# Stores of turned blocks on GpSimd, four unit buffers in the attention's first part, and adds in pieces

## The chip, the cores and the metric

The kernel runs on one core of one Trainium2 chip. The metric is device time in microseconds of one execution. A core has five engines that run side by side, each with a queue that it takes in order: TensorE (PE in the profile; it multiplies matrices, and PEld is its load of weights), VectorE (DVE), ScalarE (ACT), GpSimd (POOL) and SyncE (SP), which computes nothing and issues most transfers. Sixteen DMA engines move the data; a transfer is issued by an engine's queue, and whoever needs the data waits for its landing.

## The reference

The input x has two sequences of 2048 rows with 256 features. The layer normalises each row, and adds three things: x itself, causal attention with one head, and a feed-forward net (FFN) on the same normalised rows.

```
xn = layernorm(x)
q, k, v = xn @ Wq, xn @ Wk, xn @ Wv
out  = softmax(causal(q k^T) / 16) v @ Wo
h = silu(xn @ w1 * s1) * (xn @ w2 * s2)
h = gelu(h @ h1 * s_h1);  h = gelu(h @ h2 * s_h2)
y = x + out + (h @ w3) * s3
```

The FFN's weights hold only -1, 0 and 1 before scaling. The hidden width is 1024.

## The kernel before

**Stages.** The rows are cut into eight blocks of 512 rows (n = 0 to 7; 0 to 3 are the first sequence), and each block into four tiles of 128 rows, (n, t). The program first does the attention of all tiles, and then the FFN in four rounds of two blocks. The hidden layers of the FFN use a Strassen-like scheme of seven products each, with factors that are prepared beside the attention and kept in DRAM. Each number is carried as a high and a low part.

**A tile of the attention.** `score` (L410) multiplies the queries of a tile with the keys of each block m and moves the result to s in SBUF (L434, VectorE), and ScalarE takes the exponential (L446). These values, P, must then be turned, with the keys on partitions, before `weigh` (L505) multiplies them with the values (high parts in L518, low parts in L523) into the output bank po. There are two banks po. VectorE empties a bank into r at L537, and the next but one tile needs it.

**How P is turned.** Units of at most eight key tiles (UK = 8) go through DRAM when there are at least five key tiles in the unit (`by_blocks`, L458); smaller ones are transposed by TensorE (L490). For a unit that goes through DRAM:

1. `turn_blocks` (L305): VectorE transposes 32x32 blocks of the unit into one of two buffers b (L308), and SP stores b in DRAM as d (L313). The next but one turn waits until that store has landed, since it writes the same b.
2. `fetch_blocks` (L316): SP fetches d back with its blocks in another order, in four transfers (L320), into a buffer e. There are two buffers e, in the pool bp.
3. `turn` (L470): ScalarE casts a part of e to the high part of pT (L484), and VectorE or GpSimd subtracts it for the low part (L486; GpSimd when m is odd). There are four buffers pT.

`fetch_units` (L463) decides when a fetch is written into the program: when the first part of a unit is turned, it fetches that unit, if that is not done, and one more. The normalised x of the second sequence is turned the same way (`turn_keys`, L351), after GpSimd has normalised it (L345), 16 steps of 128 rows, in one go. Its results are the keys k (L363, L364), stored as xT_d (L365).

**Beside the attention.** Weights of the FFN are looked at, one item after another: ScalarE issues their loads, and GpSimd (L136), VectorE and ScalarE work on them. First come w1 and w2, then the signs of h2 (`item_signs`), then the factors of h1 (`item_factors`). The factors' sums are formed in xh0, a buffer of 128 x 2048 numbers that is not used earlier in the attention, and later holds the FFN's first input.

**The FFN.** A round calls `square` for h1 and for h2. After product 3 of h2, `rests_of` (L1004) loads the attention's result and x for two blocks, and GpSimd adds them (L1015), one add of 128 x 1024 numbers for each block. The last step (L1051) adds the FFN's output to that and SP stores the sum.

**Order.** The program is written in the order above, but the instructions of an engine do not stand in that order: a scheduler puts them in the order in which it expects them to become ready. `tc.issue_after(mark)` binds the instructions inside it that run on the mark's own engine to stand behind the mark; it waits for nothing. So a change in one place can move instructions of the other engines too.

Of the kernel before, what the change touches and what calls it, by code (L numbers as in the profile page):

```python
# [9 lines left out]
F32 = mybir.dt.float32  # L10
F32R = mybir.dt.float32r
# [4 lines left out]
ALU = mybir.AluOpType  # L16
# [49 lines left out]
def attn_ffn_kernel(  # L66
# [124 lines left out]
    with ExitStack() as actx:  # L191
# [6 lines left out]
        sp = actx.enter_context(tc.tile_pool(name="sp", bufs=3))  # L198
        bp = actx.enter_context(tc.tile_pool(name="bp", bufs=2))
        ptp = actx.enter_context(tc.tile_pool(name="ptp", bufs=LEAD + 2))  # L200
        small = actx.enter_context(tc.tile_pool(name="small", bufs=4))
# [3 lines left out]
        xs, rstds, ks, qs, vs = {}, {}, {}, {}, {}  # L205
        turns = {"ps": 0, "b": 0, "q": 0}

        def in_turn(key, tiles):
            turns[key] += 1
            return tiles[(turns[key] - 1) % len(tiles)]  # L210

        def bank():
# [92 lines left out]
        def turn_blocks(src, k, name):  # L305

            b = in_turn("b", b_tiles).rearrange("p i t -> p (i t)")[:, : k * P]
            nc.vector.transpose(  # L308
                b.rearrange("p (g k q) -> p k g q", g=P // Q, q=Q),
                src.rearrange("p (k g q) -> p k g q", g=P // Q, q=Q),  # L310
            )
            d = dram.tile([P, k * P], F32, name=f"d_{name}")
            nc.sync.dma_start(out=d, in_=b)  # L313
            return d
# [147 lines left out]

        def fetch_units(until, more):  # L463
            while units and (more or until not in fetched):
                more = more and until not in fetched
                n, t, u, k, d = units.pop(0)
                e = bp.tile([P, UK * P], F32, tag="e", name=f"e_{n}_{t}_{u}")[:, : k * P]
                fetched[n, t, u] = fetch_blocks(d, k, e)

        def turn(n, t, m):  # L470
# [3 lines left out]
            w = tiles * P  # L474
            pT = ptp.tile([P, 2, TB], F32R, tag="pT", name=f"pT_{n}_{t}_{m}")
            state[n, t][m] = pT
            if by_blocks(n, t, m):
                u, at = divmod((m - first) * NT, UK)
                fetch_units((n, t, u * UK), at == 0)
                src = fetched[n, t, u * UK][:, ds(at, tiles)]  # L480
                hi, lo = (
                    pT[:, a, :w].rearrange("p (k i q) -> p k i q", k=tiles, q=Q) for a in range(2)
# [146 lines left out]

        def item_signs(src):  # L630
            items.append(([src], [(0, lambda t: odd(t[0]))]))

# [17 lines left out]
        for k in range(HC):  # L650
            item_signs(h2[:, k, :])
        for c in range(HK):
# [132 lines left out]
    def ffn_ternary(actx):  # L785
# [83 lines left out]
        def square(layer, n, B, sets, last, beside):  # L869
# [6 lines left out]
            def product(step, out, start):  # L876
# [3 lines left out]
                for o in range(HK):  # L880
                    for c in range(HK):
                        for a in range(2):
                            nc.tensor.matmul(  # L883
                                out=out[o], lhsT=w[:, c, ts(o, P)], rhs=sets[right][c][:, a, :],
                                start=(start and c == 0 and a == 0), stop=(c == HK - 1 and a == 1),
                                skip_group_check=True,
                            )
                if step in beside:
# [57 lines left out]
            return C, nxt  # L946

        raw_h2 = {}

# [54 lines left out]
        def rests_of(n):  # L1004
# [4 lines left out]
            )  # L1009
            rests = {}  # L1010
            for i, m in enumerate((n + 1, n)):
                rests[m] = rest = rt[:, ts(i, NT), :]
                nc.sync.dma_start(out=rest, in_=r_d[m].rearrange("p (t d) -> p t d", d=D))
                nc.sync.dma_start(out=xt[:, ts(i, NT), :], in_=rows_of(m))
                nc.gpsimd.tensor_tensor(rest, rest, xt[:, ts(i, NT), :], ALU.add)  # L1015
            return rests

# [5 lines left out]
        for n in range(0, N, 2):  # L1023
# [6 lines left out]
            B, sets = square("h1", n, B, sets, False, later)  # L1030
            rests = {}
            B, sets = square("h2", n, B, sets, True, {3: lambda: rests.update(rests_of(n))})
            for m in (n + 1, n):
# [221 lines left out]
```

## Time and profile before

| what | us |
|---|---|
| median of 3 runs (866.09 to 869.82) | 868.33 |
| the profiled execution's own time | 868.75 |
| its span | 866.9 |
| first gated matmul of the FFN (the attention's end) | 262.2 |
| TensorE busy | 849.5 |
| GpSimd busy | 234.7 |

Busy time is the time in which an engine has an instruction in it. Matmuls overlap, so a busy TensorE is not TensorE at its peak; a gap between the starts of two matmuls that is longer than the columns of the first shows better what is lost. A bracket behind an instruction in the timeline gives the idle time of its engine before it and what ended it. The landing of a transfer is counted from its issue.

### The profile page before, as it was taken

What the parts mean: (1) busy time and instruction counts of PE and PEld (TensorE: products, weight loads), DVE (VectorE), ACT (ScalarE), POOL (GpSimd) and SP (SyncE); (2) the same over time, 40 slices, a digit from 0 to 9 for tenths busy, and PEclk for the clock granted to TensorE, in tenths of its full rate; (3) what the DMA queues carried; (4) which work ended last, traced back from release to release, by engine and by line L of the source; (5) the groups of instructions that cost most, each with busy time, mean ns of one, the idle gap of its engine ahead of it and who ended that gap; (6) DMA issues with size and microseconds to landing.
All of it is one profiled execution on the core that took longest, in us unless ns stands there. A gap on an engine that the chain in (4) does not pass through costs nothing.

```text
span 866.9 us, 12257 instructions
## 1 busy us (share of the span) xinstructions
PE 849.5 (98%) x4298; PEld 720.5 (83%) x4298; DVE 644.1 (74%) x1123; ACT 498.7 (58%) x881; POOL 234.7 (27%) x178
## 2 busy tenths in 40 slices
PE   9999799999999999999999999999999999999997
PEld 7988688988888878878988888988888898888887
DVE  6689685887965799986596596479478648848764
ACT  3456665655655466676257576436557635557671
POOL 3022823111111666630142150026024003502300
PEclk9999999999999999999999999999999999999999
DMA  8987899667881998754234444433444431144411
GB/s 276 361 233 233 249 314 291 222 234 231 286 283 51 389 403 282 285 194 152 93 132 143 144 146 141 144 116 109 145 145 145 145 135 58 49 146 146 146 49 53
DMA packets 62678, 162.51 MB, mean 187 GB/s; under 512 B 6545, under 2 KB 36369, under 8 KB 53265
## 3 DMA queue, kind: packets, MB, share of 16 engines
q1 hardware_dynamic: 57792, 145.14, 48.6%
q10 hardware_dynamic: 3728, 12.32, 4.6%
q0 software_dynamic: 1088, 4.19, 1.3%
q8 instruction: 36, 0.59, 0.3%
q14 instruction: 34, 0.27, 0.1%
HBM read 120.21 MB, written 47.71 MB: 194 GB/s over the span
## 4 chain that ended last, share of the span: by engine, by line
PE 83%; DVE 6%; DMA 5%; issue 2%; POOL 1%; ACT 1%; SPq 1%; DVEq 0%; ACTq 0%; POOLq 0%
PE ps_own L883 22%; PE ps L883 21%; PE ps L425 7%; PE ps L174 6%; PE ps_own L174 6%; PE po L518 4%; PE ps_own L1044 4%; PE ps L1044 4%; PE ps L398 3%; DMA e<-d 3%; DMA d<-b 2%; PE po L523 2%; PE ps L382 1%; POOL x L345 1%; DVE h_T L188 1%
## 5 line engine op out<-in xcount | busy, mean ns | idle before, releaser
L425 PE MATMUL ps<-k,q 128*128 128x512 f32 (+3 forms) x480 | 109.0, 366 | 0.4 <-ACT q L264 0.4
L425 PEld LDWEIGHTS ps<-k,q 128*128 128x128 f32 x480 | 82.0, 189 | 13.4 <-ACT q L264 1.2
L518 PE MATMUL po<-v,pT 128*128 128x512 f32 x272 | 79.1, 401 | 6.5 <-ACT pT L484 4.7
L486 POOL TENSOR_TENSOR pT<-e,pT 128x512 fp32r<-128x512 f32 (+3 forms) x30 | 36.8, 1229 | 140.1 <-ACT pT L484 102.6
L1015 POOL TENSOR_TENSOR rt<-rt,xt 128x1024 f32<-128x1024 f32 x8 | 21.9, 2758 | 170.3 <-issue 114.8
L904 ACT ACTIVATE k_h_u<-k_h_u,h_s_sb 128x512 f32<-128x512 f32 x64 | 45.9, 723 | 36.6 <-DVE k_h_u L903 36.0
L446 ACT ACTIVATE s<-s,low 128x1024 f32<-128x1024 f32 (+7 forms) x48 | 42.9, 895 | 30.8 <-DVE low L440 30.6
L518 PEld LDWEIGHTS po<-v,pT 128*128 128x128 f32 x272 | 47.3, 189 | 14.3 <-ACT pT L484 5.5
L863 POOL TENSOR_TENSOR k_h_u<-k_h_p,k_h_u 128x512 f32<-128x512 f32 x16 | 23.3, 1459 | 122.1 <-ACT q L187 106.0
L484 ACT CAST pT<-e 128x512 fp32r<-128x512 f32 (+3 forms) x60 | 32.8, 574 | 38.8 <-DMA e<-d 26.9
L434 DVE TENSOR_SCALAR_CACHE_REDUCE s<-ps 128x512 f32<-128x512 f32 (+3 forms) x80 | 47.2, 598 | 5.0 <-PE pt L490 3.1
L523 PEld LDWEIGHTS po<-v,pT 128*128 128x128 f32 x272 | 42.4, 188 | 6.8 <-DVE pT L486 0.7
L523 PE MATMUL po<-v,pT 128*128 128x256 f32 x272 | 46.2, 283 | 0.1
L188 DVE TENSOR_TENSOR q<-k_h_u,q 128x512 fp32r<-128x512 f32 x32 | 43.4, 1384 | 0.0
L308 DVE STREAM_TRANSPOSE b<-s 128x1024 f32<-128x1024 f32 (+3 forms) x30 | 33.4, 1124 | 8.3 <-ACT s L446 4.8
L922 POOL TENSOR_TENSOR k_h_p<-f_h_B,k_h_p 128x512 f32<-128x512 f32 x16 | 32.6, 2065 | 20.0 <-DVE h_h_T L188 20.0
L174 PE MATMUL ps<-xh,w_sb 128*128 128x512 f32 x144 | 36.4, 391 | 0.8 <-ACT b L182 0.8
L863 POOL TENSOR_TENSOR f_w_B<-f_w_B,f_w_B 128x512 f32<-128x512 f32 x16 | 26.8, 1692 | 33.1 <-DVE f_w_B L183 33.1
L903 DVE TENSOR_TENSOR k_h_u<-ps_own,k_h_u 128x512 f32<-128x512 f32 x32 | 21.7, 686 | 17.5 <-PE ps_own L883 17.4
L904 ACT ACTIVATE k_h_p<-k_h_p,h_s_sb 128x512 f32<-128x512 f32 x32 | 22.8, 722 | 19.3 <-DVE k_h_p L903 19.3
L903 DVE TENSOR_TENSOR k_h_u<-ps,k_h_u 128x512 f32<-128x512 f32 x32 | 22.0, 690 | 14.3 <-PE ps L883 14.3
L174 PE MATMUL ps<-xh1t,w_sb 128*128 128x512 f32 x128 | 31.8, 389 | 0.0
(178 smaller groups left out, 2206.2 us busy)
## 6 DMA issues: line engine op xcount, KB each, us to landing
w_h_S<-factors_h SPq DMA_DIRECT2D x32, 1024.0 KB, 4.8
w_h_A<-factors_h SPq DMA_DIRECT2D x24, 1024.0 KB, 4.8
d<-b SPq DMA_DIRECT2D x18, 512.0 KB, 3.9
e<-d SPq DMA_DIRECT2D x72, 128.0 KB, 3.2
xT_d<-k SPq DMA_DIRECT2D x8, 1024.0 KB, 6.0
stg<-in_ffn_h_w ACTq DMA_DIRECT2D x16, 512.0 KB, 4.8
r_d<-r SPq DMA_DIRECT2D x8, 512.0 KB, 4.3
factors_h<-xh SPq DMA_DIRECT2D x4, 1024.0 KB, 4.5
```

Of the source, the lines that this page charges most:

```text
L174: nc.tensor.matmul(out=p, lhsT=w[:, c, ts(o, P)], rhs=xh[:, c, a, :], start=(c == 0 and a == 0), stop=(c == DC - 1 and a == 1),)
L188: nc.vector.tensor_tensor(r[:, 1, :], f, r[:, 0, :].bitcast(F32), ALU.subtract)
L425: nc.tensor.matmul(out=ps[:, :w], lhsT=qs[n][:, c, a, ts(t, P)], rhs=ks[m][:, c, b, :w], start=(k == 0), stop=(m < n and k == 3 * DC - 1),)
L434: marks["DVE"] = nc.vector.tensor_scalar(st["s"][:, ds(at, w)], ps[:, :w], 1.0, None, ALU.mult, ALU.max, accum_out=st["tops"][:, m - first ...
L446: marks["ACT"] = nc.scalar.activation(st["s"][:, at], st["s"][:, at], AF.Exp, bias=low, accum_out=st["sums"][:, u // UK : u // UK + 1],).ins
L518: nc.tensor.matmul(out=st["po"], lhsT=pT[:, 0, ts(j, P)], rhs=vs[m][:, j, :, :], start=(m == first and j == 0), stop=False,)
L523: marks["PE"] = nc.tensor.matmul(out=st["po"][:, 0, :], lhsT=pT[:, 1, ts(j, P)], rhs=vs[m][:, j, 0, :], start=False, stop=(m == n and j == ...
L863: nc.gpsimd.tensor_tensor(B["B12"][i], B["B22"][i], B["B12"][i], ALU.subtract)
L883: nc.tensor.matmul(out=out[o], lhsT=w[:, c, ts(o, P)], rhs=sets[right][c][:, a, :], start=(start and c == 0 and a == 0), stop=(c == HK - 1 ...
L903: nc.vector.tensor_tensor(r[o], banks[o], r[o], ALU.add)
L904: nc.scalar.activation(C[k][o], r[o] if r else banks[o], AF.Gelu, scale=s[:, at : at + 1])
L1044: nc.tensor.matmul(out=ys[t][:, :D], lhsT=h[c][:, a, ts(t, P)], rhs=w3_sb[:, c, :], start=(c == 0 and a == 0), stop=(c == HC - 1 and a == 1),)
```

## The change

There are three parts.

- The store of a turned block is issued by GpSimd instead of SP (`turn_blocks`).
- The buffers e and pT are named tiles taken in turn, in place of two pools. The number of buffers pT stays. Two more buffers e lie in the halves of xh0, and are used until the last signs of h2 have been written into the program; from there on, xh0 is needed for sums, and there are two again. `fetch_units` now fetches as long as fewer than four units (or two) are fetched and not used up, at each turn and not only at a unit's first part. A unit counts as used up when its last part is turned.
- The adds of x and the attention are split into four adds of 128 x 256 for each block, and those of the two blocks are written behind products 3 and 4, inside an `issue_after` with the last matmul as its mark.

```diff
-        bp = actx.enter_context(tc.tile_pool(name="bp", bufs=2))
-        ptp = actx.enter_context(tc.tile_pool(name="ptp", bufs=LEAD + 2))
+        ptp = actx.enter_context(tc.tile_pool(name="ptp", bufs=1))
...
+        pT_tiles = [ptp.tile([P, 2, TB], F32R, name=f"pT_{i}") for i in range(LEAD + 2)]
+        e_tiles = [ptp.tile([P, UK * P], F32R, name=f"e_{i}") for i in range(2)]
+        e_more = [xh0[:, c].rearrange("p h t -> p (h t)") for c in range(DC)]
+        def units_at_once(n, t):
+            return 2 if sums_begun else 4
+        def pT_tile(n, t):
+            return in_turn("pT", pT_tiles)
+        def e_tile(n, t):
+            return in_turn("e", e_tiles + ([] if sums_begun else e_more)).bitcast(F32)
+        sums_begun = []
...
             d = dram.tile([P, k * P], F32, name=f"d_{name}")
-            nc.sync.dma_start(out=d, in_=b)
+            nc.gpsimd.dma_start(out=d, in_=b)
...
-        def fetch_units(until, more):
-            while units and (more or until not in fetched):
-                more = more and until not in fetched
+        def fetch_units():
+            while units and len(fetched) < units_at_once(*units[0][:2]):
                 n, t, u, k, d = units.pop(0)
-                e = bp.tile([P, UK * P], F32, tag="e", name=f"e_{n}_{t}_{u}")[:, : k * P]
-                fetched[n, t, u] = fetch_blocks(d, k, e)
+                fetched[n, t, u] = fetch_blocks(d, k, e_tile(n, t)[:, : k * P])
...
-                fetch_units((n, t, u * UK), at == 0)
+                fetch_units()
                 src = fetched[n, t, u * UK][:, ds(at, tiles)]
+                if at + tiles == fetched[n, t, u * UK].shape[1]:
+                    del fetched[n, t, u * UK]
...
-        def item_signs(src):
-            items.append(([src], [(0, lambda t: odd(t[0]))]))
+        def item_signs(src, last):
+            def signs(t):
+                if last:
+                    sums_begun.append(True)
+                odd(t[0])
+            items.append(([src], [(0, signs)]))
...
-                            nc.tensor.matmul(
+                            marks["PE"] = nc.tensor.matmul(
...
-                nc.gpsimd.tensor_tensor(rest, rest, xt[:, ts(i, NT), :], ALU.add)
-            return rests
+                adds[m] = [(r, r, xt[:, i * NT + t, :], ALU.add) for t in range(NT) for r in [rest[:, t, :]]]
+            return rests, adds
+        def add_rests(adds):
+            for k in adds:
+                with tc.issue_after(marks["PE"]):
+                    nc.gpsimd.tensor_tensor(*k)
...
-            B, sets = square("h2", n, B, sets, True, {3: lambda: rests.update(rests_of(n))})
+            def fetch_rests():
+                for a, b in zip((rests, adds), rests_of(n)):
+                    a.update(b)
+                add_rests(adds[n + 1])
+            B, sets = square("h2", n, B, sets, True, {3: fetch_rests, 4: lambda: add_rests(adds[n])})
```

More of the change, by code (lines that the diff above doesn't have):

```diff
@@ L205, in attn_ffn_kernel @@
         xs, rstds, ks, qs, vs = {}, {}, {}, {}, {}
-        turns = {"ps": 0, "b": 0, "q": 0}
+        turns = {"ps": 0, "b": 0, "q": 0, "pT": 0, "e": 0}
         def in_turn(key, tiles):
@@ L210, in in_turn @@
             return tiles[(turns[key] - 1) % len(tiles)]
+        pT_tiles = [ptp.tile([P, 2, TB], F32R, name=f"pT_{i}") for i in range(LEAD + 2)]
+        e_tiles = [ptp.tile([P, UK * P], F32R, name=f"e_{i}") for i in range(2)]
+        e_more = [xh0[:, c].rearrange("p h t -> p (h t)") for c in range(DC)]
+        assert UK * P == 2 * TB == NT * D
+        def units_at_once(n, t):
[5 more added lines that the diff above has]
+        sums_begun = []
         def bank():
@@ L474, in turn @@
             w = tiles * P
-            pT = ptp.tile([P, 2, TB], F32R, tag="pT", name=f"pT_{n}_{t}_{m}")
+            pT = pT_tile(n, t)
             state[n, t][m] = pT
@@ L650, in attn_ffn_kernel @@
         for k in range(HC):
-            item_signs(h2[:, k, :])
+            item_signs(h2[:, k, :], k == HC - 1)
         for c in range(HK):
@@ L886, in product @@
                                 skip_group_check=True,
-                            )
+                            ).ins
                 if step in beside:
@@ L946, in square @@
             return C, nxt
+        marks = {}
         raw_h2 = {}
@@ L1009, in rests_of @@
             )
-            rests = {}
+            rests, adds = {}, {}
             for i, m in enumerate((n + 1, n)):
@@ L1030, in ffn_ternary @@
             B, sets = square("h1", n, B, sets, False, later)
-            rests = {}
-            B, sets = square("h2", n, B, sets, True, {3: lambda: rests.update(rests_of(n))})
+            rests, adds = {}, {}
+            def fetch_rests():
[3 more added lines that the diff above has]
+            B, sets = square("h2", n, B, sets, True, {3: fetch_rests, 4: lambda: add_rests(adds[n])})
             for m in (n + 1, n):
```

## The prediction

> **What bounds the kernel now.** Read first: the page's busy times.
>
> ```profile
> span 866.9 us, 12257 instructions
> ...
> PE 849.5 (98%) x4298; PEld 720.5 (83%) x4298; DVE 644.1 (74%) x1123; ACT 498.7 (58%) x881; POOL 234.7 (27%) x178
> ```
>
> TensorE bounds the program, and it is idle for only 17.4 us. From 422 us on, the windows show it busy 146.00 of 146 us in a round of the FFN. So a gain has to come out of TensorE's gaps in the attention. I listed from the timeline every place where the next matmul starts later than the matrix columns explain. Three places lose over 2 us, and a few others about 1 us. The table of windows around the three (each cell is busy us and count, then granted clock, DMA share, GB/s):
>
> ```profile
> core 0: us, PE busy (x) PEld busy (x) DVE busy (x) ACT busy (x) POOL busy (x), PEclk, DMA share, GB/s
> 84.00:90.00 6.00, 3.96 (x22) 3.19 (x21) 3.33 (x7) 4.28 (x8) 3.31 (x6) 1.00 0.94 256
> ...
> 102.00:106.00 4.00, 1.39 (x10) 1.19 (x9) 1.51 (x3) 2.65 (x5) 2.71 (x2) 1.00 1.11 254
> ...
> 135.00:139.00 4.00, 2.12 (x12) 1.67 (x11) 4.00 (x9) 0.00 (x0) 0.00 (x0) 1.00 0.86 300
> 139.00:143.00 4.00, 4.00 (x22) 3.62 (x20) 2.48 (x8) 2.86 (x6) 0.00 (x0) 0.57 1.02 274
> ```
>
> The next matmul is late by 2.41 us at 86.6, 2.78 us at 102.9 and 2.06 us at 135.9. After the third, the granted clock falls: it is one half for 3.41 us, another 1.7 us. Together 8.95 us.
>
> The first one, in the timeline:
>
> ```profile
> 77.84 1.05 POOL L136 TENSOR_SCALAR w_sb<-stg 128x1024 fp32r<-128x1024 f32 x1 [11.44 <-DMA stg<-in_ffn_w_w]
> ...
> 80.18 4.59 SPq L320 DMA_DIRECT2D e<-d  x8
> ...
> 89.21 1.21 PE L518 MATMUL po<-v,pT 128*128 128x512 f32 x4 [2.04 <-ACT pT L484]
> ...
> 91.98 0.34 SPq L313 DMA_DIRECT2D d_x<-b  x1
> ```
>
> SP fetched tile (3,0) only at 80.18, though its store had landed at 69.8. Both e buffers still held tile (3,1), whose last GpSimd subtractions (78.86 to 81.31) stood behind a weight copy that waited 11.44 us for a load. The second one, in the chain of waits:
>
> ```profile
> 90.35 6.80 POOL x L345 x8
> 97.15 1.26 POOL pT L486
> ...
> 99.72 5.25 DMA e<-d
> ```
>
> Tile (2,3) was fetched from 98.43 on, because its buffer was released by a subtraction that ran behind 14 normalisations. Both are waits for an e buffer. The third is not:
>
> ```profile
> 134.96 1.25 DVE L308 STREAM_TRANSPOSE b<-x 128x1024 f32<-128x1024 f32 x1 [4.26 <-DMA d<-b]
> ...
> 138.44 0.77 PE L518 MATMUL po<-v,pT 128*128 128x512 f32 x2 [1.89 <-DVE r L537]
> ```
>
> VectorE stood 4.26 us before a turn, because the store out of that b buffer took 6.4 us to land, and what TensorE needed (r) stood behind the turn.
>
> What a store costs on either queue, from the DMA issues and from the records of line L967, the only stores that GpSimd issues now:
>
> ```profile
> d<-b SPq DMA_DIRECT2D x18, 512.0 KB, 3.9
> ...
> factors_h<-xh SPq DMA_DIRECT2D x4, 1024.0 KB, 4.5
> ...
> factors_h<-stgt_h POOLq DMA_DIRECT2D x4, 1024.0 KB, 7.9
> ```
>
> ```profile
> L967 POOL DMA_DIRECT2D factors_h<-stgt_h x4: 769/769/943, 297.9 to 338.3; - x4
> ...
> DMA to landing us min/median/max: 5.7/7.9/11.0
> ```
>
> The first 769-943 ns is GpSimd's own time for one store; SP's issue takes 338 ns and costs no engine. For the same 1 MB, GpSimd's landed after 5.7 to 11.0 us, SP's after 4.5. The two longest (9.8, 11.0) were issued while the DMA engines were 96% busy; the two after 320 us took 6.1 and 5.7.
>
> **The change part by part.** The sum is made against the profiled execution, 868.75 us (span 866.9 and 1.85 around it); the median of the runs shown is 868.33, 0.42 lower.
>
> *Four buffers.* Until the last item of h2's signs, two more e buffers lie in xh0, so a fetch no longer waits for the tile two before. At 86.6: tile (3,0)'s store landed at 69.8 and can be fetched at once; its first fetch row took 4.3 us to land and the last 6.6, ScalarE's cast 0.62, so it is there before 80, and TensorE comes at 86.6. Gain 2.41. At 102.9: tile (2,3)'s store landed at 82.53, its buffer frees at 81.31, so it can be fetched from 83 to 85 and lands by 90; in the changed order of instructions the matmuls that want it stand 7.8 us of columns earlier, near 91. Just in time; gain 2.78.
>
> *Stores on GpSimd.* SP's 34 issues (0.34 us each) go; it waited 30.2 us there on VectorE, and the fetches that stood behind move up. GpSimd takes 34 x 0.77 = 26.2 us more. It is busy for 63.4 us of the 238 between 40 and 278, so its idle time hides them; with that cover gone, each would delay a subtraction by 0.77 us. But GpSimd takes its queue in order, and four places need a price:
>
> (a) The last part of tile (3,0) needs a GpSimd subtraction that stands behind a store, one longer subtraction and 12 normalisations. The store's turn ended at 85.71; 85.7 + 0.77 + 0.56 + 1.28 = 88.3; the 12 take 0.56 (most rows) to 0.75 us (the mean of the 14 from 86.69 to 97.12): 95.0 to 97.3; plus 0.46: 95.5 to 97.7. TensorE is there at 95.3: tile (3,0) begins at 86.6, and 8.7 us of columns stand between in the changed order. A new stall of 0.2 to 2.4 us; I take 1.0, nearer the low end, as ten of the 14 ran at 0.56.
>
> (b) The store of x block 4, issued at 91.98 by SP, now stands behind the rest of the normalisations and a subtraction: 96.5 + 3 x 0.67 + 1.3 = 99.8. It lands 4.8 us (SP's median for such blocks) to 5.9 us after its 0.77: 105.4 to 106.5. Tile (1,2)'s turn waits for that buffer; the other buffer is waited for too (a subtraction and a store later: 107.4 to 108.5), and behind both turns stand 1.25 + 1.2 + 0.7 + 0.5 us of VectorE's work up to the r that frees the output bank of tile (2,1): 111.1 to 112.2. TensorE reaches it at 119.3 before; less 2.41 and 2.78, less 1.8 of columns moved, plus (a): 113.3; by its columns alone, counted from tile (3,0), it would be there at 109.8. So from on time to 2.4 late; I take 0.5, as the measured arrival is the nearer row.
>
> (c) At 135.9 two buffers still serve the turns. Now one more turn (block x 4) falls into the stretch from 100 to 136, nine in place of eight. The wait for x block 7 remains in some form: from nothing to what it costs now with the slow clock (2.06 + 1.7). I take 1.2: TensorE's order has that matmul 1.8 us of columns later, which uses up most of 2.06.
>
> (d) From 160 us on there are two e buffers, as before. A store costs 0.44 us more to issue and lands 1.2 us later (5.7 against 4.5). Three units have no slack there: the cast ends at 192.02, 262.62 and 268.52, and TensorE takes it 0.1 to 0.3 us later. From -1.3 (the loss at 260.4 goes, because a store is no longer behind a 1 MB load in SP's queue: one landed 10.2 us after its issue at 239.5) to 3 x 1.64 = 4.9. I take 0.5, as most units have 3 to 6 us of slack.
>
> [...]
>
> *The adds.* In the order of instructions the four pieces stand in the very places of each whole add; the mark is a TensorE instruction and binds nothing on GpSimd. A whole add takes 2.76 us. A piece lies between 0.56 (a 128x256 scaling) and 1.2 us (a 128x256 subtraction), four of them 2.2 to 4.8. In three of four rounds GpSimd was idle for over 54 us before them, which hides it. In the first, adds ran at 358.84 and 367.06, and TensorE lost 0.59 + 1.13 us at 369.7 to 372.2 with VectorE's subtractions at 1.7 us beside them: from -1.7 to +2.0. I take 0, the order being the same.
>
> Sum: 868.75 - 8.95 + 1.0 + 0.5 + 1.2 + 0.5 = 863.0; by the median 862.6.
>
> **Rivals.** *Swapped stalls (0.30).* The upper ends of (a) to (c): -8.95 + 2.4 + 2.4 + 3.8 = -0.35, some 868.0. For it: VectorE's waits for b are 10.6 us in six places, and four e buffers do nothing for them. Against: the two waits for e are certain to go.
>
> *Slower (0.15): the turn buffers become the bound.* Between 100 and 136 us nine turns share two buffers, so 36 us leave 8.0 us for each: 1.25 turn, 0.85 issue, 5.9 landing. Above that, each us costs 4.5. SP's take 3.9 to 4.8, GpSimd's quiet ones 5.7, its slowest 11.0. It decides against the change at 5.9 + (5.75 + 4.3) / 4.5 = 8.1 us. At 8.5 us the program takes 868.33 - 5.75 + 11.7 = 874.3; at 11.0 885. For it: the DMA engines are 86 to 102% busy there. Against: these stores are half as big as the measured ones.
>
> *The change doesn't do what it says:* the adds are not ordered by the mark, as told; that moves 0 to 2 us and decides nothing.
>
> **How the numbers follow.** Forecast 862.6 with chance 0.55, own range 857 to 865. Lowest: 868.33 - 8.95 - 1.3 - 1.7 = 856.4. The range goes up into the slower case, to 874, with some 0.12 above and 0.05 below. A difference under 0.5% (4.3 us) is about what a measurement of this kernel cannot tell from none. Faster, under 864.0: 0.53 (nearly all of the first case). Within: 0.31. Slower: 0.16, the last rival and a little of the second.
>
> **What would show it.** TensorE's next matmuls at 86.6 and 102.9 on time, casts waiting less for e (26.9 us now). d stores on the software queue, 34 of about 0.77 us on GpSimd, landing within 6 us. VectorE's wait for b (10.6 us) about the same or some more; if over 20 us, the slower rival. No half clock near 139. The span up to the first gated matmul (262.2 now) near 256.5. Wrong if stores land over 8 us after issue, if GpSimd's queue holds back its subtractions, or if the FFN moves by over 2 us.

## The result, and the profile after

The changed kernel takes 871.49 us (median of 20 runs, 867.05 to 876.16); the kernel before, run beside it, takes 867.33 us (20 runs, 863.11 to 870.52). The ratio is 1.0049 [1.0034, 1.0064]: 0.5% slower. The forecast was 862.6 us, faster. The direction was wrong; the range, up to 874, held the time.

The profiled execution of the changed kernel took 876.16 us, 4.7 us above its own median, so its stretches show where time is lost rather than exactly how much. Its page:

```profile
span 874.4 us, 12342 instructions
...
PE 852.8 (98%) x4298; PEld 722.9 (83%) x4298; DVE 644.1 (74%) x1123; ACT 499.7 (57%) x881; POOL 261.3 (30%) x236
...
d<-b POOLq DMA_DIRECT2D x18, 512.0 KB, 4.4
```

GpSimd is busy 26.6 us more, and the span is 7.5 us longer. To say where, I use a sum that I call TensorE's loss: over neighbouring matmuls, the time from one's start to the next's start, less 0.4427 ns for each column of the first. That is what a column takes where matmuls follow each other without a gap: the starts of neighbouring matmuls of 512 columns are most often 226 or 227 ns apart. It holds gaps and stretches of slow clock alike. "After, again" is a second profile of the changed kernel. Two experiments (told below) run the instructions of the attention in exactly the order of the kernel before, so their losses show how far one profile scatters.

| loss in us, by when | 0-80 | 80-160 | 160-280 | from 280 | all |
|---|---|---|---|---|---|
| before | 9.7 | 14.1 | 7.3 | 8.0 | 39.1 |
| same order: adds alone | 10.4 | 16.6 | 8.8 | 6.2 | 42.0 |
| same order: pT by hand | 10.8 | 17.9 | 8.5 | 6.2 | 43.4 |
| after | 10.1 | 18.4 | 12.4 | 5.7 | 46.6 |
| after, again | 10.7 | 17.2 | 11.5 | 6.3 | 45.7 |

Against the mean of the three with the old order, the two profiles of the changed kernel lose 1.6 us more from 80 to 160 (17.8 against 16.2), where 6.2 was to be won, and 3.8 more from 160 to 280 (12.0 against 8.2), where 0.5 had been set. The 1.6 is no more than the three differ among themselves (14.1 to 17.9); that nothing was won there, and the 3.8, are clear. Before 80 and from 280 on they lose no more than the others.

The windows around the forecast's three places (columns as before: busy us and count of PE, PEld, DVE, ACT, POOL, then granted clock, DMA share, GB/s), with one further on:

```profile
84.00:90.00 6.00, 4.36 (x24) 3.48 (x23) 4.42 (x11) 5.90 (x11) 2.54 (x4) 1.00 0.83 277
...
102.00:106.00 4.00, 3.85 (x23) 3.50 (x24) 0.67 (x1) 3.85 (x8) 3.97 (x7) 1.00 0.24 47
135.00:139.00 4.00, 4.00 (x31) 3.75 (x30) 3.49 (x15) 2.82 (x6) 1.00 (x1) 1.00 1.00 331
...
142.00:150.00 8.00, 4.49 (x23) 3.83 (x22) 5.10 (x9) 6.40 (x14) 6.87 (x7) 0.81 0.98 324
```

The gap of 135 to 139 is gone, and the one near 103 too. The one near 87 stays, and a larger one, with slow clock behind it, has come at 144. The timeline shows each.

**Near 87: the fetch is early, the matmul is late all the same.**

```profile
72.72 3.63 SPq L337 DMA_DIRECT2D xh<-d  x8
...
81.19 1.05 POOL L136 TENSOR_SCALAR w_sb<-stg 128x1024 fp32r<-128x1024 f32 x1 [3.40 <-DMA stg<-in_ffn_w_w]
...
82.22 1.27 POOL L504 TENSOR_TENSOR pT<-e,pT 128x512 fp32r<-128x512 f32 x1
82.27 1.77 DVE L614 TENSOR_SCALAR stg<-stg 128x1024 uint32<-128x1024 uint32 x1 [1.23 <-POOL w_sb L136]
...
84.07 1.06 ACT L616 ACTIVATE stg<-stg 128x1024 f32<-128x1024 uint32 x1 [3.23 <-DVE stg L614]
...
85.99 0.69 DVE L614 TENSOR_SCALAR stg<-stg 128x1024 uint32<-128x1024 uint32 x1 [0.70 <-POOL w_sb L136]
...
88.84 0.62 ACT L502 CAST pT<-xh 128x512 fp32r<-128x512 f32 x1
...
89.52 1.22 PE L536 MATMUL po<-v,pT 128*128 128x512 f32 x4 [1.64 <-ACT pT L502]
```

Tile (3,0) is fetched from 72.72 on, 7.5 us sooner than before, and has landed by 81.33. ScalarE's cast of it begins only at 88.84 and waits for nothing then: the work ahead of it in ScalarE's queue has run late. That queue stood still for 3.23 us before a look at w2 (L616), which waited for VectorE's look, which waited for GpSimd's copy, which waited for the load of w2. TensorE loses 1.85 us here, against 2.26 before (the forecast's 2.41 has three short transposes ahead of it as well).

VectorE's look is itself longer than its work: 1.77 us here, and 0.69 for the next one at 85.99. A GpSimd subtraction began 0.05 us before it (82.22), and the look ended 0.55 us after that. It is so in every profile: all 31 looks of this kind that began during a GpSimd subtraction ended 0.55 to 0.56 us after it, after 0.72 to 1.78 us, and those without one took 0.65 to 0.70.

The kernel before, at the same cast:

```profile
80.74 1.06 ACT L598 ACTIVATE stg<-stg 128x1024 f32<-128x1024 uint32 x1 [1.98 <-DVE stg L596]
...
88.54 0.62 ACT L484 CAST pT<-e 128x512 fp32r<-128x512 f32 x1 [1.71 <-DMA d<-b]
```

There ScalarE was idle for 1.71 us before the cast, because the fetch landed last (its fourth part at 88.36; the stores, to which the bracket puts the wait down, had landed by 83.84). So even without the fetch the cast could have come at most 1.71 us earlier, unless its queue moved too.

**Near 101: the normalisations, as in term (a).**

```profile
92.39 9.28 POOL L362 TENSOR_SCALAR x<-x,rstd,off 128x256 f32<-128x256 f32 x12
...
96.61 1.23 DVE L325 STREAM_TRANSPOSE b<-x 128x1024 f32<-128x1024 f32 x1
...
101.64 0.45 POOL L504 TENSOR_TENSOR pT<-xh,pT 128x128 fp32r<-128x128 f32 x1
...
102.15 0.39 PE L541 MATMUL po<-v,pT 128*128 128x256 f32 x1 [1.40 <-POOL pT L504]
...
104.91 0.61 POOL L330 DMA_DIRECT2D d_x<-b  x1
```

Twelve normalisations stand ahead of the subtraction that TensorE needs: 1.56 us are lost. The store of x block 4 is issued at 104.91, though its turn ended at 97.84: it was held for 7.1 us in GpSimd's queue. Meanwhile the DMA engines are busy to a quarter (the window from 102).

**Near 144: a late fetch, and an engine that waits for it.**

```profile
133.06 2.99 SPq L337 DMA_DIRECT2D x<-d_x  x4
...
141.78 1.25 DVE L325 STREAM_TRANSPOSE b<-x 128x1024 f32<-128x1024 f32 x1 [1.56 <-DMA d<-b]
...
142.25 0.62 ACT L380 CAST k<-x 128x512 fp32r<-128x512 f32 x1 [3.57 <-DMA x<-d_x]
...
147.06 0.47 DVE L555 SCALAR_TENSOR_TENSOR r<-po,inv,y 128x256 f32<-128x256 f32 x1
...
147.59 2.07 PE L536 MATMUL po<-v,pT 128*128 128x512 f32 x4 [3.51 <-DVE r L555]
```

ScalarE stood 3.57 us before the keys' cast, because x block 5, turned at 124.64, stored at 126.93 and fetched from 133.06, landed at 142.18. In the kernel before it was turned at 117.84 and fetched by 127.58. Here the turn came 6.8 us later, and the transfers were slower, with the DMA engines 98 to 100% busy in the two windows above: the store landed after 5.8 us (4.2 before), and the fetch took 9.1 us (4.2 before). The store had left 1.06 us after the turn, so GpSimd's queue is a small part of it. What TensorE needed (r, at 147.06) came behind that: 3.73 us.

**Near 272: an order of ScalarE's.**

```profile
270.04 1.28 ACT L182 ACT_TABLE_LOAD   x1
...
271.33 0.69 ACT L182 ACTIVATE b<-ps,w_s_sb 128x512 f32<-128x512 f32 x1
271.92 1.13 ACT L502 CAST pT<-e 128x512 fp32r<-128x512 f32 x2
...
272.58 1.51 PE L536 MATMUL po<-v,pT 128*128 128x512 f32 x4 [1.97 <-ACT pT L502]
```

The FFN's first activation (L182), with a table load of 1.28 us, stands right ahead of a cast that TensorE is about to need: 2.13 us. In the kernel before the same two stand where TensorE has transposes to do, and it loses 0.98 there.

What the forecast had feared did not come. VectorE's waits for b, from the list of waits, have gone down from 10.6 us to 3.7, and GpSimd's stores are cheaper than the ones that had been measured (the last line is for all 34 of them):

```profile
ACT pT L502 <- DMA e<-d: 27.1, 12, 6.6
...
DVE b L325 <- DMA d<-b: 3.7, 3, 1.6
```

```profile
L330 POOL DMA_DIRECT2D d<-b x30: 533/564/742, 39.7 to 259.6; - x30
...
DMA to landing us min/median/max: 3.0/4.8/7.5
```

The casts wait for e as long as before (27.1 us against 26.9), with twice as many buffers, and 10.9 us of waits for units in xh0 come on top. One of them is new to TensorE: at 122.12 a cast had waited 4.71 us for a fetch whose last part took 9.1 us to land, and behind it TensorE lost 1.73 us at 123.2 (0.95 in the second profile).

### The profile page after: what moved, and what is told of

Its sections match the earlier page's. It is cut to its first block, busy times and chain, and to the rows that moved or that the text cites. A ratio compares the mean times of both kernels' runs of the same rounds, so it can differ in the third digit from the quotient of the medians.

```text
span 874.4 us, 12342 instructions
## 1 busy us (share of the span) xinstructions
PE 852.8 (98%) x4298; PEld 722.9 (83%) x4298; DVE 644.1 (74%) x1123; ACT 499.7 (57%) x881; POOL 261.3 (30%) x236
## 4 chain that ended last, share of the span: by engine, by line
PE 74%; DMA 11%; DVE 4%; issue 4%; SPq 3%; POOL 2%; ACT 2%; ACTq 0%; POOLq 0%; DVEq 0%
PE ps_own L906 22%; PE ps L906 22%; PE ps L174 6%; PE ps_own L174 5%; DMA d<-b 4%; PE ps_own L1080 4%; PE ps L1080 4%; PE po L536 3%; PE ps L442 3%; DMA e<-d 3%; SPq L337 2%; PE po L541 1%; DMA xh<-d 1%; DMA x<-d_x 1%; PE ps L399 1%
## 5 line engine op out<-in xcount | busy, mean ns | idle before, releaser
L442 PEld LDWEIGHTS ps<-k,q 128*128 128x128 f32 x480 | 82.1, 189 | 15.1 <-ACT q L281 3.0
L536 PE MATMUL po<-v,pT 128*128 128x512 f32 x272 | 81.9, 410 | 9.3 <-ACT pT L502 4.5
L1046 POOL TENSOR_TENSOR rt<-rt,xt 128x256 f32<-128x256 f32 x32 | 31.4, 1017 | 165.8 <-DMA xt<-in_attn_x 108.4
L536 PEld LDWEIGHTS po<-v,pT 128*128 128x128 f32 x272 | 48.3, 193 | 18.4 <-ACT pT L502 5.7
L463 ACT ACTIVATE s<-s,low 128x1024 f32<-128x1024 f32 (+7 forms) x48 | 42.9, 896 | 26.7 <-DVE low L457 26.6
L541 PEld LDWEIGHTS po<-v,pT 128*128 128x128 f32 x272 | 43.4, 193 | 9.7 <-POOL pT L504 2.6
L330 POOL DMA_DIRECT2D d<-b x30 | 17.3, 576 | 103.4 <-DVE total L547 46.9
L502 ACT CAST pT<-e 128x512 fp32r<-128x512 f32 (+3 forms) x44 | 24.2, 579 | 32.5 <-DMA e<-d 27.1
L504 POOL TENSOR_TENSOR pT<-e,pT 128x512 fp32r<-128x512 f32 (+3 forms) x22 | 26.7, 1212 | 35.0 <-ACT pT L502 34.8
L188 DVE TENSOR_TENSOR h_h_B<-f_h_B,h_h_B 128x512 fp32r<-128x512 f32 x32 | 21.4, 717 | 14.8 <-ACT h_h_B L187 14.8
```

What stands on the lines that cost most here:

```text
L188: nc.vector.tensor_tensor(r[:, 1, :], f, r[:, 0, :].bitcast(F32), ALU.subtract)
L442: nc.tensor.matmul(out=ps[:, :w], lhsT=qs[n][:, c, a, ts(t, P)], rhs=ks[m][:, c, b, :w], start=(k == 0), stop=(m < n and k == 3 * DC - 1),)
L463: marks["ACT"] = nc.scalar.activation(st["s"][:, at], st["s"][:, at], AF.Exp, bias=low, accum_out=st["sums"][:, u // UK : u // UK + 1],).ins
L536: nc.tensor.matmul(out=st["po"], lhsT=pT[:, 0, ts(j, P)], rhs=vs[m][:, j, :, :], start=(m == first and j == 0), stop=False,)
L541: marks["PE"] = nc.tensor.matmul(out=st["po"][:, 0, :], lhsT=pT[:, 1, ts(j, P)], rhs=vs[m][:, j, 0, :], start=False, stop=(m == n and j == ...
```

## The experiments

Each ratio is to the kernel before, run on the same chip, with its 95% interval.

### One part at a time

The four buffers e, with pT and e as named tiles, without the other two parts (here against the changed kernel):

```diff
-            nc.gpsimd.dma_start(out=d, in_=b)
+            nc.sync.dma_start(out=d, in_=b)
...
-                with tc.issue_after(marks["PE"]):
-                    nc.gpsimd.tensor_tensor(*k)
+                nc.gpsimd.tensor_tensor(rest, rest, xt[:, ts(i, NT), :], ALU.add)
```

> The kernel before with the four e buffers alone (stores stay on SP's queue, the adds whole). Theory G (in the changed kernel GpSimd holds back: the store of x block 4 left 7.1 us after its turn, behind twelve normalisations, and all that needs it comes late, up to the stall of 3.7 us at 143.8 with half a clock after it): without stores on GpSimd the gain is there and the loss is not, so 0.990 to 0.997 of before, no stall over 2 us at 86.6 and 102.9, and x block 4 stored within 2 us of its turn. Theory B (the four buffers themselves cost: fetches come earlier and crowd the DMA engines, and the planned order is worse): 1.002 to 1.010 of before. Theory L (stores on the software queue land later): as G.

The stores alone:

```diff
-            nc.sync.dma_start(out=d, in_=b)
+            nc.gpsimd.dma_start(out=d, in_=b)
```

> The kernel before with the stores on GpSimd alone (two e buffers, the adds whole). Theory G: x block 4's store is again held over 5 us behind normalisations, and the stalls for an e buffer stay: 1.004 to 1.012 of before. Theory B: 0.998 to 1.002. Theory L: 1.004 to 1.012 as G, but with stores that leave within 1.5 us of their turns and land later than SP's by 1.5 us or more.

The adds alone (the last part of the change, as in the diff above):

> The kernel before with the adds in pieces alone. All theories: the attention is as before, its order being the same. The FFN of the changed kernel's profile lost 3.2 us less than before's; if that is the pieces' doing, 0.996 to 0.9985 of before and the two losses of 0.59 and 1.13 us near 370 go; if it is scatter, 0.999 to 1.001.

And the changed kernel with the stores of the x blocks back on SP:

```diff
-            nc.gpsimd.dma_start(out=d, in_=b)
+            (nc.sync if name.startswith("x_") else nc.gpsimd).dma_start(out=d, in_=b)
```

> The changed kernel with only the four stores of x blocks back on SP's queue; the 30 of the P units stay on GpSimd. Theory G: x block 4 is stored within 2 us of its turn, the stall near 143.8 and its half clock (5.4 us together) go, those near 100 and 107 (2.7 us) may stay: 0.993 to 0.999 of before. Theory L: 30 of 34 stores still land late: 1.003 to 1.007. Theory B: 1.003 to 1.007.

| kernel | ratio | profiled span | loss 80-160 | 160-280 |
|---|---|---|---|---|
| four buffers, named tiles | 1.0048 [1.0025, 1.0071] | 874.2 | 14.3 | 14.9 |
| stores on GpSimd | 1.0023 [1.0005, 1.0041] | 867.9 | 15.1 | 9.4 |
| adds in pieces | 0.9984 [0.9969, 1.0000] | 869.9 | 16.6 | 8.8 |
| changed, x blocks stored by SP | 1.0100 [1.0073, 1.0127] | 876.7 | 16.5 | 14.6 |

The part that was to bring all of the gain costs 0.5% by itself, without a store being moved. The stores on GpSimd cost 0.2%. The adds cost nothing, and perhaps gain a little. Added up, the three parts give 1.0055, against 1.0049 for the whole. Sending the x blocks by SP did not cure the stall near 144 (3.2 us at 146.55), so GpSimd's queue is not what makes that block late; the kernel got slower.

### Named tiles without any new buffer

The first part also replaces pools by named tiles. This alone, for pT, leaves the number of buffers, their use and every store as before:

```diff
-        ptp = actx.enter_context(tc.tile_pool(name="ptp", bufs=LEAD + 2))
+        ptp = actx.enter_context(tc.tile_pool(name="ptp", bufs=1))
+        pT_tiles = [ptp.tile([P, 2, TB], F32R, name=f"pT_{i}") for i in range(LEAD + 2)]
...
-            pT = ptp.tile([P, 2, TB], F32R, tag="pT", name=f"pT_{n}_{t}_{m}")
+            pT = in_turn("pT", pT_tiles)
```

> The kernel before with one thing changed: the four buffers pT are named tiles taken in turn in place of a pool of four. Number and size of the buffers stay, as do two e buffers, SP's stores and whole adds; but 208 of VectorE's instructions stand in other places. Theory O (the part of the change that costs is this one: taken in turn, the pT buffers give the scheduler another order, above all from 160 us on): 1.004 to 1.010 of before, with 4 to 8 us more lost on TensorE between 160 and 280 us. Theory F (the four e buffers or the new fetch rule cost): 0.999 to 1.001. Theory S (GpSimd's stores cost): 0.999 to 1.001.

The other way round, pT comes from a pool again, once in the kernel with four buffers and once in the changed kernel, which was also run a second time:

> Four e buffers alone as in the run before, but with the pT buffers in the pool again (stores on SP, adds whole). Theory O: the loss after 160 us goes, 0.993 to 1.000 of before. Theory F: 1.003 to 1.009, as with pT by hand (1.0048). Theory S: 0.990 to 0.998.

> The changed kernel with the pT buffers in the pool again; four e buffers, GpSimd's stores and the adds in pieces stay. Theory O: 0.993 to 1.000 of before. Theory F and theory S: 1.003 to 1.008, as the changed kernel.

> The changed kernel once more, beside the other three on one chip: 1.003 to 1.0065 of before by all theories. Its second profile tells which of the stalls stand in every execution: if the stall of 3.7 us near 144 with half a clock after it is systematic it is there again; what is lost from 160 to 280 us (13.3 us in the first profile, 7.2 in before's) should be over 11 again by theories O and F.

| kernel | ratio | profiled span | loss 80-160 | 160-280 |
|---|---|---|---|---|
| pT by hand, two e | 1.0045 [1.0028, 1.0063] | 877.8 | 20.4 | 12.4 |
| four e, pT from a pool | 1.0091 [1.0063, 1.0118] | 876.8 | 14.9 | 16.7 |
| changed, pT from a pool | 1.0049 [1.0029, 1.0069] | 872.1 | 13.0 | 14.9 |
| changed, again | 1.0032 [1.0017, 1.0047] | 873.8 | 17.2 | 11.5 |

An edit that adds no buffer and moves no transfer to another queue costs as much as the whole change. What it does alter is the order that the scheduler makes: 208 of VectorE's instructions stand elsewhere, and at 422 of TensorE's 4298 places the trace has another matmul (by tile and size) than the kernel before. Pools are no remedy (the second and third row): with other edits beside it, the same pool gives yet another order. The timeline of the kernel with pT by hand shows one place of the kind:

```profile
141.21 1.25 DVE L310 STREAM_TRANSPOSE b<-x 128x1024 f32<-128x1024 f32 x1 [4.37 <-DMA d<-b]
142.38 0.52 DVE L436 TENSOR_SCALAR_CACHE_REDUCE s<-ps 128x384 f32<-128x384 f32 x1
...
142.97 1.42 PE L400 MATMUL ps<-wvo,k 128*128 128x256 f32 x7 [4.05 <-DVE s L436]
```

A turn that waits 4.37 us for a store stands ahead of a score's copy that frees a bank, and TensorE waits for that copy.

### Each part in the order of before

If it is the order, each part must lose its cost when the order of before is kept. At the attention's end, every engine gets a list of its instructions, as they stand in the kernel before, and each is queued behind the one ahead of it in the list. That binds the order; in the first row of the table below a kernel so bound, with pT by hand, takes 0.9995 [0.9977, 1.0013] of before, so no cost of the binding itself shows. A store that has moved to GpSimd has no place in these lists; where it stands there is left to the scheduler:

```diff
+def in_order(tc, nc):
+    traced = [i for i in nc.cur_bb.bb.instructions if type(i).__name__ != "BassTilePoolBoundary"]
+    for name, runs in ORDER.items():
+        mine = [i for i in traced if str(i.engine) == f"EngineType.{name}"]
...
+        for a, b in zip(mine, mine[1:]):
+            tc.add_manual_dep(b, a.name, ...)
```

> The kernel with the pT buffers as named tiles, and every instruction of the attention on all five engines held in the order that it has in the kernel before. Theory P (what costs is the other order of instructions that the scheduler makes of each edit; the named tiles themselves cost nothing): 0.9985 to 1.0015 of before, against 1.0045 without the order held. Theory R (the buffers themselves: taken strictly in turn, a pT buffer is waited for while another is free): 1.003 to 1.006.

> Four e buffers (and pT as named tiles), stores on SP, whole adds, and the attention held in the order of the kernel before on all engines. Theory P: the fetches come earlier at least where SP was free, and nothing is later: 0.993 to 1.000 of before, against 1.0048 without the order held; the losses at 86.6 and 102.9 get smaller only if the fetches, which stand in SP's queue as before, move up. Theory R: 1.003 to 1.007.

> GpSimd's stores alone (two e buffers), with the attention held in the order of the kernel before on all engines; only the places of the stores among GpSimd's instructions are the scheduler's. Theory P: the store of x block 4 is still held behind normalisations, so 0.999 to 1.004 of before (1.0023 without the order held). Theory R (GpSimd's stores cost by themselves, by holding back subtractions): 1.002 to 1.006.

> The whole change (four e buffers, GpSimd's stores, adds in pieces), with the attention held in the order of the kernel before. Theory P: the stall of 3.7 to 4.7 us near 144 goes and what is lost from 160 to 280 us is under 9 us (11.5 to 12.4 in the two profiles of the changed kernel): 0.992 to 0.999 of before. Theory R: 1.002 to 1.007, as the changed kernel (1.0049, 1.0032).

| kernel, in the order of before | ratio | same edit, scheduler's order |
|---|---|---|
| pT by hand | 0.9995 [0.9977, 1.0013] | 1.0045 [1.0028, 1.0063] |
| four buffers, named tiles | 0.9998 [0.9979, 1.0016] | 1.0048 [1.0025, 1.0071] |
| stores on GpSimd | 1.0132 [1.0101, 1.0164] | 1.0023 [1.0005, 1.0041] |
| whole change | 1.0116 [1.0086, 1.0146] | 1.0049 [1.0034, 1.0064] |

For the named tiles this is the answer: the order costs 0.5%, and nothing else in them does. (With the order kept, TensorE's trace has the same matmul as the kernel before at all 4298 places.) The four buffers, once the order is kept, neither gain nor lose. That is the second finding, and the more awkward one: 5.2 us of the forecast's gain rested on them. For the whole change the answer is not as clean, since it gets slower in the old order, not faster.

The two with stores on GpSimd are slower in this order, and the timeline of the stores alone (GpSimd, SP and TensorE) shows why:

```profile
88.21 8.42 POOL L411 TENSOR_SCALAR x<-x,rstd,off 128x256 f32<-128x256 f32 x14 [0.94 <-DVE off L366]
...
101.27 0.61 POOL L379 DMA_DIRECT2D d_x<-b  x1
...
104.31 1.81 SPq L386 DMA_DIRECT2D x<-d_x  x4
...
113.65 1.65 PE L584 MATMUL po<-v,pT 128*128 128x512 f32 x3 [6.37 <-ACT pT L550]
```

The turn of x block 4 ended at 95.29. Its store was issued at 101.27, behind the normalisations and two subtractions; the fetch, another fetch behind it on SP, the keys and a cast of pT followed, and TensorE lost 6.5 us there (8.1 us with the whole change). In the scheduler's own order the same edit costs 0.2%.

### Why four buffers gain nothing

With the order of all engines but SP kept, SP may issue the fetches as soon as it can. And since the normalisations stood ahead of a subtraction in both kernels, GpSimd may do those of blocks 5 to 7 later. The diff of the second is one line of GpSimd's list (numbers count its instructions as the program writes them); the third has both, with one more subtraction moved ahead of block 4's keys:

```diff
-38-41 44-51 55-56 34 57-58 35 53-54 36-37 42-43 60-61
+38-41 34-35 44-47 53-54 36-37 42-43 48-51 55-58 60-61
```

> Four e buffers, stores on SP, whole adds; TensorE, VectorE, ScalarE and GpSimd held in the order of before, and only SP's queue left to the scheduler, so that fetches move ahead of stores (tile (3,0)'s fetch stands ahead of the store of tile (2,3), which was behind it). With SP held too, the run gave 0.9998 and still lost 2.8 us near 87. Theory S (the gain of the four buffers is real, and it was SP's order that kept it away): the stall near 87 goes, 0.995 to 0.9985 of before. Theory Q: 0.9985 to 1.002.

> The kernel before, held in its own order on all engines, but GpSimd normalises x blocks 5, 6 and 7 later: two subtractions (for tile (3,0)) come straight after x block 4, then block 5, and blocks 6 and 7 after the subtraction for tile (2,0). Nothing else differs. Theory N (twelve normalisations ahead of those subtractions make the stall at 102.9, by holding an e buffer): most of its 2.78 us goes, 0.995 to 0.9985 of before. Theory Q (the b buffers and the DMA engines set the pace there, so what is gained is lost at the next wait): 0.9985 to 1.002.

> Four e buffers with SP's queue free, and GpSimd's later normalisations (the subtraction for tile (2,3) also ahead of the keys of x block 4); TensorE, VectorE and ScalarE held in the order of before, stores on SP, whole adds. Theories N and S: both stalls go, 0.990 to 0.996 of before. Theory Q: 0.998 to 1.002.

> The whole change (four e buffers, GpSimd's stores, adds in pieces), with TensorE, VectorE and ScalarE held in the order of before, SP's queue free, and GpSimd's order given by hand: normalisations later as above, each store at the place where its turn ends in the profile of before. The whole change in before's order gave 1.0116, with 8.1 us lost at one place near 106. Theory N (that place waits for x block 4's store, which stood behind the normalisations): the 8.1 us go, 0.992 to 1.000 of before. Theory L (stores on GpSimd cost by themselves, wherever they stand): over 1.005.

| kernel | ratio | loss 80-160 | 160-280 |
|---|---|---|---|
| four buffers, SP free | 0.9996 [0.9974, 1.0018] | 15.3 | 8.3 |
| two buffers, normalisations later | 0.9998 [0.9979, 1.0017] | 15.4 | 8.9 |
| both | 1.0011 [0.9991, 1.0032] | 17.6 | 7.0 |
| whole change, SP free, normalisations later, stores at their turns | 1.0063 [1.0040, 1.0085] | 19.7 | 8.5 |

None gains. In the first, tile (3,0) is fetched early, and its first part had landed at 76.56, its second at 80.9. TensorE still lost 2.44 us. The timeline (GpSimd, VectorE, ScalarE) is the same chain as in the changed kernel:

```profile
80.51 1.06 POOL L199 TENSOR_SCALAR w_sb<-stg 128x1024 fp32r<-128x1024 f32 x1 [14.22 <-DMA stg<-in_ffn_w_w]
...
81.60 1.77 DVE L677 TENSOR_SCALAR stg<-stg 128x1024 uint32<-128x1024 uint32 x1 [3.19 <-POOL w_sb L199]
...
83.41 1.06 ACT L679 ACTIVATE stg<-stg 128x1024 f32<-128x1024 uint32 x1 [4.62 <-DVE stg L677]
...
89.40 0.60 ACT L565 CAST pT<-xh 128x512 fp32r<-128x512 f32 x1
```

The load of w2 that this chain waits for was issued at 74.23 and landed at 80.44; in the kernel before it was 73.83 to 77.76. So the fetch goes earlier, into the time of this load, and the load takes 6.2 us in place of 3.9. In the two profiles of the changed kernel, where the fetch is early too, it takes 5.2 and 4.9; in five others, where it comes later or has nearly landed by then, 3.6 to 3.7. The cast stands behind the look in ScalarE's queue, and gains nothing.

With the normalisations later, the other stall shows its second leg:

```profile
92.03 1.78 POOL L554 TENSOR_TENSOR pT<-e,pT 128x512 fp32r<-128x512 f32 x2
...
93.15 1.25 DVE L376 STREAM_TRANSPOSE b<-x 128x1024 f32<-128x1024 f32 x1 [2.59 <-DMA d<-b]
...
98.98 5.20 SPq L388 DMA_DIRECT2D e<-d  x8
...
107.75 1.63 PE L586 MATMUL po<-v,pT 128*128 128x512 f32 x3 [2.71 <-ACT pT L552]
```

The subtractions that free the buffer end at 93.8, yet the fetch goes out at 98.98, when it did before (98.43): in SP's queue it stands behind the fetch of x block 4 (97.13), and that waits for the block's store (94.42), which waits for its turn, which waited 2.59 us for the b buffer. 2.88 us are lost, against 2.78. With both edits the first place shows the queue alone: the fetch of tile (3,0) had landed by 77.14 and the load took 3.6 us, yet the cast began at 88.64, without a wait, behind a look at the next weight (87.58), and TensorE still lost 1.50 us. The other stall moves again, to 99.15, where TensorE waited 4.76 us for a score's copy behind a turn that waited 6.15 us for a store to land.

In the last row the 8.1 us of the whole change in the old order are gone, which fits stores late behind normalisations; SP's order was free as well in this run, so that is not shown apart. 0.6% remain, spread over places of 1 to 3 us (2.99 us at 153.1 is the largest): 12.5 us are lost before 80, where before loses 9.7. That fits the theory by which stores on GpSimd cost by themselves, wherever they stand (over 1.005), but I have not taken the waits apart.

### Fewer bytes

If the transfers themselves, not the buffers, set the pace there, less traffic must gain where more buffers did not. The ten loads of w2 and of h2's signs bring an eighth of their bytes (seven eighths of these weights are left out, so the FFN's numbers are others), in the order of before, with two e buffers in the first and with four and the later normalisations in the second. The two buffers that these loads fill are named tiles here:

```diff
+                    part = SC // 8 if 2 <= i < 2 * DC + HC else SC
-                    nc.scalar.dma_start(out=t, in_=src)
+                    nc.scalar.dma_start(out=t[:, :part], in_=src[:, :part])
```

> The kernel before, held in its own order on all engines, but the ten weight loads that ScalarE issues for w2 and for h2's signs (512 KB each, some 75 to 150 us) bring an eighth of their bytes. The looks and copies of these weights run as before on what is in the buffer; seven eighths of w2 are left out, so the FFN's numbers are others, and the attention's are not. Theory W (these loads set the losses around 87 and 103: they land late beside the blocks' transfers, and GpSimd's copy, VectorE's look and ScalarE's look, behind which ScalarE's cast for tile (3,0) stands, wait for them): over 3 us less lost between 80 and 160 us (14.1 in before's profile), 0.990 to 0.997 of before. Theory B2 (the turned blocks' own way through DRAM with two b buffers sets the pace): 0.998 to 1.001.

> The same short loads with four e buffers, SP's queue free and the later normalisations (the run before with both gave 1.0011). Theory W: with the loads out of the way the four buffers show their gain: at least 2 us under the short loads alone, 0.985 to 0.994 of before. Theory B2: as the short loads alone within 1 us, or 0.998 to 1.002.

| kernel | ratio | loss 80-160 | mean landing of transfers issued 80-160 |
|---|---|---|---|
| before | 1 | 14.1 | 4.76 |
| short loads, two e | 0.9908 [0.9885, 0.9931] | 8.0 | 3.86 |
| short loads, four e, normalisations later | 0.9922 [0.9900, 0.9944] | 7.6 | 3.38 |
| after | 1.0049 [1.0034, 1.0064] | 18.4 | 5.01 |

ScalarE and the window from 80 to 100 with short loads and two buffers:

```profile
79.28 1.06 ACT L671 ACTIVATE stg<-stg 128x1024 f32<-128x1024 uint32 x1 [0.29 <-DVE stg L669]
...
85.27 0.61 ACT L557 CAST pT<-e 128x512 fp32r<-128x512 f32 x1
```

```profile
80.00:100.00 20.00, 19.84 (x106) 16.38 (x105) 14.43 (x34) 13.30 (x24) 14.55 (x19) 1.00 0.57 160
```

The stalls near 87 and 136 are gone with two e buffers, the one near 103 is down from 2.78 to 1.35 us, and TensorE is busy 19.84 of 20 us from 80 to 100. Four buffers add nothing to that: 0.9922 against 0.9908, with intervals that overlap. So the traffic is the cause of some 6 us of loss in this stretch. This run changes two things at once, how late the looks are and how long every other transfer takes to land, and it does not tell their shares apart; for the place near 87, the chain of the looks does.

## Why the prediction was wrong

**"Gain 2.41" (at 86.6): wrong.** The forecast was right that tile (3,0) would be fetched at once and land before 82. It was wrong that the matmul would then be on time, because it followed the data as far as the landing, added the cast's 0.62 us, and did not ask what stands ahead of the cast on ScalarE. A look at w2 did. 1.85 us are still lost; with the old order, 2.44. In the kernel before, ScalarE had been idle for only 1.71 us before that cast, so 2.41 was never to be had from the fetch alone. The line with "11.44 <-DMA stg<-in_ffn_w_w" was even among those quoted. It was read, rightly, as the reason why a buffer came free late; but the same load also holds back the look, and with the buffer there it holds the matmul up by that way.

**"Gain 2.78" (at 102.9): eaten up.** The next unit's fetch was issued from 83.51, as forecast, and with it that stall is gone. But 1.56 us were lost to term (a) just ahead of it, and 1.11 more at 107, where ScalarE's cast had waited 1.94 us for the same subtraction. Of the gain 0.1 us is left. In the old order the stall stays with the buffer freed sooner, because the fetch is third in a row on SP.

**The third stall (2.06 us and 1.7 of slow clock, less term (c)'s 1.2): moved.** At 135 to 139 TensorE is never idle and the clock is 1.00. What replaced it, 3.73 us at 143.8 with the clock at 0.81 in its window, has another cause than (c)'s: not a turn that waits for a buffer, but keys that wait for x block 5, which in the new order is turned 6.8 us later, and whose store and fetch take 15.3 us in place of 8.5. Without the slow clock it is already near (c)'s upper end of 3.8.

**(a), 1.0 us, from 0.2 to 2.4: right in kind and size.** 1.56 us, at the place named.

**(b), 0.5 us: the cause was there, its effect not.** The store of x block 4 was issued at 104.91, 5.1 us later than the forecast had it. But TensorE lost nothing near 113, and the waits for b that were to carry the delay did not come.

**(d), 0.5 us, up to 4.9: undersized.** The stretch lost 3.8 us more. The upper bound had the right size but largely the wrong reason: one of its three units (named at 262.62) was late with a cast that waited for its fetch, by 0.38 us in the first profile and 1.34 in the second. The 2.13 us at 270.4 (2.20 in the second) come from the order on ScalarE, for which no term had been set. The pT-by-hand kernel, with no store moved, loses 12.4 in this stretch as well, and with the order of before 8.5.

**The adds at 0, from -1.7 to 2.0: right.** Alone 0.9984 [0.9969, 1.0000]. From 280 us on, the runs with adds in pieces lose 5.6 to 6.5 us, those with whole adds 5.9 to 8.0.

**The missing term.** The forecast used the new order for where instructions stand, and priced the change's parts in it. It set nothing for the new order as such: instructions that no part of the change touches, but that stand elsewhere. The experiments put 0.45 to 0.5% on that for the named tiles alone, some 4 us, which is the size of the whole result. With both gains at about nothing, the sum would have been 868.75 - 3.76 + 3.2 = 868.2 without that term (867.8 by the median), "the same"; with 4 us for it, 871.8 by the median, against 871.49 measured. This is a sum after the fact, and its parts are not independent.

**The rivals.** "Swapped stalls" named the right outcome (new waits where old ones went), by other waits than it named. "Slower" was to come from landings of over 8.1 us out of b; the median landing of a 512 KB store was 4.4 us and the longest 7.5, and VectorE waited less for b than before. Its outcome came, its mechanism did not. Of the signs listed, "casts waiting less for e" failed plainly.

**What stays open.** Which of the moved instructions cost the 0.5% is shown only at single places (near 142 and 272). How much of the whole change's 0.5% is order is not shown by itself: its four-buffer part alone loses its 0.5% when the order is kept, but the stores cost more there. What the whole change costs in the old order with late normalisations, 0.6%, is not taken apart either. No version beat the kernel before by more than its interval, short of leaving bytes out.

## What to carry to other kernels

Follow a late matmul back through the queue of each engine and not along its data alone: here an operand that had landed by 81.33 was cast only at 88.84, behind what stood ahead of it, and two buffers more gained nothing (0.9998 in the old order) while that queue ran late. Where a scheduler orders the instructions, price an edit twice, once as such and once for the order that it brings about; to measure the two apart, keep the old order by hand. And before adding buffers in a stretch where the DMA engines are busy, look at what the earlier transfers will delay: with four buffers fetched early, the load of w2 took 6.2 us here in place of 3.9.

## What the runs showed of the hardware

- A store issued by GpSimd cost that engine 0.56 us (533 to 742 ns), less than the 0.77 us of the four 1 MB stores, and 512 KB landed after a median of 4.4 us, near SP's 3.9. So the price of the larger stores did not hold for these.
- A store of GpSimd's can end late beside one of VectorE's looks (128x1024 uint32): the store at 83.44 ran beside the look that ended at 84.04, and ended itself at 84.16, after 0.72 us. In the eight profiles with these stores on GpSimd, 16 stores ended 0.12 us after a look, after 0.59 to 1.02 us. Three others, beside a look that ended sooner, took 0.55 to 0.61, and nearly all the rest 0.53 to 0.62. It met one to three stores of a profile's 30 or 34. What holds a store there is not shown.
- A look that began during a GpSimd subtraction ended 0.55 to 0.56 us after it, in 31 of 31 cases, and took up to 1.78 us in place of 0.69. This is part of the chain near 87.
- Ten weight loads cut to an eighth made the program 0.9% faster, though none of them feeds a matmul of that stretch: the mean landing of the transfers issued from 80 to 160 us went from 4.76 to 3.86 us (from 4.70 to 3.89 without ScalarE's weight loads).
